# Edge layer of a four-layer image kernel: a quarter of one term on ScalarE, made a block ahead; the rest shared between VectorE and GpSimd

## The chip, the cores and the metric

The kernel runs on one core of a Trainium2 chip. A core has five engines with their own instruction queues: TensorE (PE in the profile, its weight loads PEld), VectorE (DVE), ScalarE (ACT), GpSimd (POOL) and SyncE (SP), which issues DMAs. Each queue runs in its own order, and an instruction waits until what it reads has been written and what it overwrites has been read. The metric is the device time of one execution in microseconds (us); shorter is better.

## The reference, cut to what matters

The program adds four layers to an image x of 4 x 56 x 56 x 128 numbers, each after a group norm. The change lies in the second layer alone:

```python
def _L1_conv_ref(x, We, be, Wn, bn):
    f = x.shape[-1]
    W1, W2 = (We[:, :f], We[:, f:])
    proj_i = jnp.einsum('blnf,of->blno', x, W1)
    proj_j = jnp.einsum('blnf,of->blno', x, W2)
    edge = jax.nn.relu(proj_i[:, :, :, None, :] + proj_j[:, :, None, :, :] + be)
    edge_sum = edge.sum(axis=3)
    node_in = jnp.concatenate([x, edge_sum], axis=-1)
    node = jax.nn.relu(jnp.einsum('blnc,oc->blno', node_in, Wn) + bn)
    return node
...
x = x + _L1_conv_ref(_gn(x), L1_conv_We, L1_conv_be, L1_conv_Wn, L1_conv_bn)
```

For every pixel n of an image row l and every of the 56 pixels m of the same row, an edge relu(proj_i[n] + proj_j[m] + be) is formed for each of 128 channels, and the edges are summed over m. That is 56 times as many numbers as the image has, so the work of the layer is in the element-wise edges and their sum.

## The kernel before, in words

The four samples go through the first two layers one after the other: `fast_layer` (layer 0) and then `edge_layer` (layer 1), four times each. `edge_layer` takes a sample as 7 blocks (`NBLK`) of 8 image rows, that is 448 pixels (`NB`). In a block the 128 channels are cut into four rows r of 32 channels, and the 56 partners m into four quarters of 14 (`M`), which lie on the four groups of 32 partitions. So one tile "128 x 1792" holds, for one m out of 14, all four rows r (4 x 448 elements) and on its partitions 32 channels for four partners at once. A block needs 14 such terms, and these are the 14 turns of the string `EDGE_TURNS` (`EDGE_END` in the last block).

- `project(j)`, TensorE: `e_pa`, the first projection of block j (four banks, one per row r), and `e_pc`, the negated second one.
- `evacuate(j, part)`, ScalarE: copies of these into SBUF, `e_a` (with the bias be added) and `e_c`; part 1 also adds bn to the sample (L1263).
- `terms(j, m, t, r0, r1, e)`: one term or some of its rows. For "d" VectorE forms max(a, c) in one instruction (L1273, tile `e_td`), reading c from PSUM. For "p" GpSimd forms a - c (L1275, tile `e_tp`) and ScalarE takes the relu in place (L1277). Since max(a, c) = relu(a - c) + c, what VectorE's terms have too much is summed per block into `e_rest` (two reduces, L1366 and L1367) and taken off by a matmul (L1360).
- A turn "s" is shared: rows 0 and 1 on VectorE (128 x 896), rows 2 and 3 on GpSimd and ScalarE.
- After each turn four matmuls per term (one per row r, L1344) sum it into `e_acc`, over partitions with a matrix of ones on four diagonals.
- At the end of a block ScalarE copies `e_acc` to `e_sums` (L1369), TensorE forms the node projection (`begun`, L1285, and `output`, L1291), and `finish` (L1296, VectorE) adds its relu to the sample. `finish(j - 2)` stands in VectorE's queue after turn 3 of block j, and in the last block `finish(j - 1)` after turn 9.
- `normed(j + 2)`, ScalarE, at turn 10: the group norm of a block to come (L1231).

`EDGE_TURNS` "ddpddpsdpdpddp" has 8 d, 5 p and 1 s; `EDGE_END` "ddpddpdpdpdddd" has 10 d and 4 p. Turns are counted from 0, so the p turns of a block are 2, 5, 8, 10 and 13; this text calls them p2 to p13, and s(j) is the shared turn (6) of block j.

The order on TensorE, ScalarE and VectorE is the order of the program text (`manual_schedule`). GpSimd's is not fixed by hand: the scheduler sets it. VectorE's full tiles have 7 buffers, GpSimd's 4, and the tiles of a shared turn 2.

Of the kernel before, what the change touches and what calls it, by code (L numbers as in the profile page):

```python
# [12 lines left out]
F32 = mybir.dt.float32  # L13
AF = mybir.ActivationFunctionType
ALU = mybir.AluOpType
AX = mybir.AxisListType
# [3 lines left out]
P = 128  # L20
B = 4
HH = 56
TOK = HH * HH
NB = 448
NBLK = TOK // NB
# [7 lines left out]
def bc(ap, axis, n):  # L33

    ap = ap.unsqueeze(axis)
    shape = list(ap.shape)
    shape[axis] = n
    return ap.to_broadcast(shape)


def blk(j):
    return slice(j * NB, (j + 1) * NB)
# [149 lines left out]
def apply_norm(k, out, xt, mr):  # L192
    k.nc.vector.tensor_scalar(out, xt, mr[:, 0:1], mr[:, 1:2], ALU.subtract, ALU.mult)
# [1004 lines left out]

EDGE_TURNS, EDGE_END = "ddpddpsdpdpddp", "ddpddpdpdpdddd"


def edge_layer(k, w, x1, st):
# [6 lines left out]
    nc, tc = k.nc, k.tc  # L1211
# [3 lines left out]
    with ExitStack() as es:  # L1215
        big = es.enter_context(tc.tile_pool(name="e_big", bufs=1))
        wk = es.enter_context(tc.tile_pool(name="e_wk", bufs=2))
# [7 lines left out]
        ready = {}  # L1225

        def normed(j):
            if j < 2:
                apply_norm(k, xg[:, blk(j)], xf[:, blk(j)], mr)
            elif j < NBLK:  # L1230
                nc.scalar.activation(xg[:, blk(j)], xf[:, blk(j)], AF.Identity, bias=shift, scale=mr[:, 1:2])  # L1231
# [22 lines left out]
        def evacuate(j, part):  # L1254
            if j >= NBLK:
                return
            pc, pa, c, a = ready[j]
            for r in range(2 * part, 2 * part + 2):
                nc.scalar.activation(a[:, r, :], pa[r][:, :NB], AF.Identity, bias=w.be[:, r:r + 1])
                if r == 0:  # L1260
                    nc.scalar.copy(c.rearrange("p r l m -> p (r l m)"), pc[:, :NB])  # L1261
            if part == 1:
                nc.scalar.activation(xf[:, blk(j)], xf[:, blk(j)], AF.Identity, bias=w.bn)  # L1263

        def terms(j, m, t, r0, r1, e):

            pc, _, c, a = ready[j]
            if e == "d":
                c = pc[:, :NB].rearrange("p (r l m) -> p r l m", r=4, l=8)
            cm = bc(c[:, r0:r1, :, m], 3, HH)  # L1270
            am = a[:, r0:r1, :].rearrange("p r (l n) -> p r l n", l=8)
            if e == "d":
                nc.vector.tensor_tensor(t, am, cm, ALU.max)  # L1273
            else:
                nc.gpsimd.tensor_sub(t, am, cm)  # L1275
                tf = t.rearrange("p r l n -> p (r l n)")
                nc.scalar.activation(tf, tf, AF.Relu)  # L1277

        def tile_of(e, n=4):
            return wk.tile([P, n, 8, HH], F32, tag="e_%s%d" % (e, n), name="e_t" + e,  # L1280
                           bufs=2 if n < 4 else 7 if e == "d" else 4)
# [16 lines left out]
        with tc.manual_schedule(engines={mybir.EngineType.PE, mybir.EngineType.Activation, mybir.EngineType.DVE}):  # L1298
            idle = psum.tile([P, 512], F32, tag="e_pc", name="e_idle", bufs=2)

            def fill(n):

                for _ in range(n):
                    nc.tensor.matmul(idle[:, :3 * P], k.ident, bc(k.ones, 1, 3), start=True, stop=True)
            mr = group_norm_factors(k, wk, bank, st, fill)
            nc.vector.tensor_scalar(shift, mr[:, 0:1], mr[:, 1:2], -1.0, ALU.mult, ALU.mult)
            for j in range(2):
                normed(j)
            project(0)
            for part in range(2):  # L1310
                evacuate(0, part)
            project(1)
            last = po = None
            for j in range(NBLK):
                end = j == NBLK - 1
                turns = EDGE_END if end else EDGE_TURNS
                nd, ns = turns.count("d"), turns.count("s")
                acc = psum.tile([P, 512], F32, name="e_acc")
                rest = wk.tile([P, 4, 8], F32, name="e_rest")
                at, ms = {"d": 0, "p": nd + ns, "s": nd}, []  # L1320
                for e in turns:
                    ms.append(at[e])
                    at[e] += 1
                early = {}
                if j == 0:
                    early = {g: tile_of(turns[g]) for g in
                             [g for g, e in enumerate(turns) if e == "d"][:3] + [turns.index("p")]}
                    for r in range(4):
                        for g, t in early.items():
                            terms(j, ms[g], t[:, r:r + 1], r, r + 1, turns[g])  # L1330
                for g, e in enumerate(turns):
                    m = ms[g]
                    if g in early:
                        parts = [(early[g], 0)]
                    elif e == "s":
                        parts = [(tile_of("d", 2), 0), (tile_of("p", 2), 2)]
                        for t, r in parts:
                            terms(j, m, t, r, r + 2, "p" if r else "d")
                    else:
                        parts = [(tile_of(e), 0)]  # L1340
                        terms(j, m, parts[0][0], 0, 4, e)
                    for t, r0 in parts:
                        for r in range(t.shape[1]):
                            nc.tensor.matmul(acc[quarters[r0 + r], :NB], w.S[:, 0, :], t[:, r].rearrange("p l n -> p (l n)"),  # L1344
                                             start=(g == 0), stop=(g == len(turns) - 1))
                    if g == 3 and po is not None:
                        finish(j - 2, po)
                    if g == 5:
                        evacuate(j + 1, 0)
                    if g == 7:  # L1350
                        evacuate(j + 1, 1)
                    if g == 10:
                        normed(j + 2)
                    if g == 6 and end:
                        po = output(*last)
                    if g == 9 and end:
                        finish(j - 1, po)
                    if g == 11:
                        for r in range(4):
                            nc.tensor.matmul(acc[quarters[r], :NB].rearrange("p (l n) -> p l n", l=8), w.S[:, 1, :],  # L1360
                                             bc(rest[:, r, :], 2, HH), start=False, stop=False)
                        if end:
                            po = begun(j)
                    if g == 8:
                        if ns:
                            nc.vector.tensor_reduce(rest[:, 0:2], ready[j][2][:, 0:2, :, 0:nd + 1], AX.X, ALU.add)  # L1366
                        nc.vector.tensor_reduce(rest[:, 2 if ns else 0:4], ready[j][2][:, 2 if ns else 0:4, :, 0:nd], AX.X, ALU.add)  # L1367
                sums = wk.tile([P, NB], F32, name="e_sums")
                nc.scalar.copy(sums, acc[:, :NB])  # L1369
                if end:  # L1370
                    idle = psum.tile([P, 512], F32, tag="e_pc", name="e_idle", bufs=2)
                    fill(2)
                if last and not end:
                    po = output(*last)
                project(j + 2)
                last = j, sums
            po = output(*last, po)
            fill(2)
            finish(NBLK - 1, po)
# [1476 lines left out]
def group_norm_factors(k, pool, bank, st, fill):  # L2856

    nc = k.nc
    mv = pool.tile([P, 2], F32, tag="mv", name="gf_mv")
    nc.vector.bn_aggr(mv, st.rearrange("p a b -> p (a b)"))  # L2860
    ps = bank()
    fill(2)
    nc.tensor.matmul(ps[:, 0:1], k.g4, mv[:, 0:1], start=True, stop=True)
    fill(1)
    mr = pool.tile([P, 2], F32, tag="mr", name="gf_mr")
    nc.vector.tensor_copy(mr[:, 0:1], ps[:, 0:1])
    t = pool.tile([P, 1], F32, tag="gt", name="gf_t")
    nc.vector.tensor_sub(t, mv[:, 0:1], mr[:, 0:1])
    nc.vector.tensor_mul(t, t, t)
    nc.vector.tensor_add(t, t, mv[:, 1:2])  # L2870
    ps = bank()
    nc.tensor.matmul(ps[:, 0:1], k.g4, t, start=True, stop=True)
    fill(1)
    nc.scalar.activation(t, ps[:, 0:1], AF.Sqrt, bias=k.eps)
    nc.vector.reciprocal(mr[:, 1:2], t)
    return mr
# [176 lines left out]
```

## Time and profile before

| What | Value |
|---|---|
| median of three runs | 3445.36 us (3444.44 to 3445.95) |
| the profiled execution: its time | 3443.31 us |
| the profiled execution: its span | 3441.5 us |
| mean granted TensorE clock | 0.997 |
| the four edge layers (from the first term to the last output) | 132.24, 132.19, 132.16, 132.30 us |
| busy per edge layer, mean: PE, DVE, ACT, POOL | 124.67, 125.56, 89.32, 120.11 us |

The span is what the profiler saw between the first and last instruction; the execution's own time has 1.8 us more around it. In the first sample the layer runs from 543.83 to 676.07 us; the blocks' first sums start at 549.69, 569.21, 588.94, 607.97, 625.76, 643.55 and 656.67 us. The other three samples show the same pattern within a few hundredths of a microsecond, so one is read and counted four times. A line of the timeline gives the start in us, the busy time in us, engine, source line, operation, output and inputs with their shapes, how many instructions were merged in the line, and in brackets the idle time before it with what ended it. Successive instructions on an engine overlap a little (a full tile's 3.26 us on POOL come 3.22 us apart, ScalarE's 1.70 us ones 1.60), so distances of starts are used where several follow each other.

### The profile page before, as it was taken

The page shows a single profiled execution, that of the slowest core. Times are in us where ns is not written, and L with a number is a line of the kernel's source. Part 1 is how long each engine was busy: PE and PEld are TensorE (multiplying, and loading weights), DVE is VectorE, ACT ScalarE, POOL GpSimd, SP SyncE. Part 2 cuts the span into 40 slices and gives each one's busy share as a digit, 9 for nine tenths or more (in the row PEclk, how much of TensorE's full clock was granted, in tenths as well). Part 3 has the DMA queues.
Part 4 walks back from the last instruction along what each step waited for, and adds up shares of the span by engine and source line. Part 5 has one row for each costly group of instructions (what it writes and reads, how often), then busy time and mean ns, then how long its engine had stood idle before and what let it go on. Part 6 is the DMA issues. An engine that isn't in the chain of part 4 may idle for free. (4 is left out here: it accounts for less than half of the span.)

```text
span 3441.5 us, 64526 instructions
## 1 busy us (share of the span) xinstructions
PE 3317.2 (96%) x27834; PEld 1425.6 (41%) x27834; DVE 2651.4 (77%) x2552; ACT 2134.0 (62%) x2257; POOL 1284.9 (37%) x795
## 2 busy tenths in 40 slices
PE   7999999999999999999999999999999999999998
PEld 4433333353333435333343443333437443336664
DVE  6588877867888597788859858887785878895776
ACT  4688876668888575788867668887564013215442
POOL 1000007800000491000019500000685978884786
PEclk9999999999999999999999999999999999999999
DMA  2143420024344000444320034442104047743111
GB/s 107 45 93 90 97 54 20 20 51 96 88 93 89 20 1 20 102 97 97 87 48 5 20 74 93 97 91 61 38 12 110 2 96 186 189 112 94 57 20 57
DMA packets 97868, 243.42 MB, mean 71 GB/s; under 512 B 64440, under 2 KB 69816, under 8 KB 92440
## 3 DMA queue, kind: packets, MB, share of 16 engines
q0 software_dynamic: 16128, 102.77, 14.9%
q1 hardware_dynamic: 74728, 123.61, 12.3%
q10 hardware_dynamic: 6720, 12.85, 1.4%
q8 instruction: 220, 3.60, 0.4%
q14 instruction: 72, 0.59, 0.1%
HBM read 79.43 MB, written 31.33 MB: 32 GB/s over the span
## 5 line engine op out<-in xcount | busy, mean ns | idle before, releaser
L830 ACT ACTIVATE f_ring<-f_pm 128x1792 f32<-128x1792 f32 (+1 forms) x764 | 1093.8, 1482 | 226.6 <-PE f_pm L827 179.1
L682 DVE TENSOR_TENSOR f_acc<-f_acc,f_ring 128x1792 f32<-128x1792 f32 x468 | 947.7, 2025 | 191.4 <-ACT f_ring L830 161.1
L827 PE MATMUL f_pm<-f_qT,f_kT 32*128 32x448 f32 x5376 | 722.8, 571 | 9.9 <-ACT f_p L716 4.1
L672 POOL DMA_DIRECT2D f_far<-f_ring x112 | 96.5, 862 | 1327.5 <-ACT f_ring L830 1012.3
L693 PE MATMUL f_pm<-f_ring,f_va 128*32 128x448 f32 (+1 forms) x6304 | 589.4, 490 | 0.0
L1275 POOL TENSOR_TENSOR e_tp<-e_a,e_c 128x1792 f32<-128x1792 f32 (+2 forms) x172 | 480.3, 2833 | 33.4 <-issue 33.4
L1273 DVE TENSOR_TENSOR e_td<-e_a,e_pc 128x1792 f32<-128x1792 f32 (+2 forms) x292 | 478.4, 1706 | 8.8 <-ACT e_c L1261 8.8
L827 PEld LDWEIGHTS f_pm<-f_qT,f_kT 32*128 32x128 f32 x5376 | 260.1, 183 | 411.8 <-ACT f_ring L830 301.1
L693 PEld LDWEIGHTS f_pm<-f_ring,f_va 128*32 128x32 f32 x6304 | 163.9, 109 | 410.1 <-issue 397.8
L1277 ACT ACTIVATE e_tp<-e_tp 128x1792 f32<-128x1792 f32 (+2 forms) x172 | 253.3, 1495 | 98.0 <-POOL e_tp L1275 98.0
L2040 DVE TENSOR_TENSOR u_ud<-u_px,u_d 112x1792 f32<-112x1792 f32 x144 | 263.5, 1863 | 39.9 <-PE u_po L2045 35.4
L2042 POOL TENSOR_TENSOR u_up<-xh,u_d 112x1792 f32<-112x1792 f32 (+1 forms) x72 | 240.9, 3374 | 56.0 <-PE u_po L2045 39.7
L1344 PE MATMUL e_acc<-e_td,t_edge 128*32 128x448 f32 x1952 | 231.6, 542 | 6.6 <-DVE e_td L1273 6.4
L2045 PE MATMUL u_po<-u_ud,AT 112*64 112x448 f32 x1056 | 212.4, 541 | 0.5 <-DVE u_ud L2040 0.5
L1344 PE MATMUL e_acc<-e_tp,t_edge 128*32 128x448 f32 x1184 | 148.0, 543 | 23.6 <-ACT e_tp L1277 23.6
L2045 PEld LDWEIGHTS u_po<-u_ud,AT 112*64 112x64 f32 x1056 | 74.0, 137 | 126.5 <-issue 112.6
L1344 PEld LDWEIGHTS e_acc<-e_td,t_edge 128*32 128x32 f32 x1952 | 61.8, 110 | 142.4 <-issue 93.8
L737 DVE RECIPROCAL f_den<-f_den 128x448 f32<-128x448 f32 x28 | 82.6, 2951 | 44.5 <-ACT f_den L734 44.5
L1874 POOL TENSOR_TENSOR q_u<-iS,q_g 128x1792 f32<-128x1792 f32 x32 | 104.3, 3287 | 12.2 <-PE q_acc L1889 12.2
L813 POOL TENSOR_TENSOR x<-xf,xw 128x343 f32<-128x343 f32 x28 | 25.5, 909 | 222.1 <-DVE xf L802 222.1
L2145 ACT COPY x_ev<-x_po 56x896 f32<-56x896 f32 x32 | 28.8, 900 | 125.1 <-DMA x_xs<-xat 69.9
L1889 PE MATMUL q_acc<-q_u,S 64*64 64x448 f32 x1024 | 101.2, 540 | 2.1 <-DVE y L1908 1.1
(535 smaller groups left out, 4575.7 us busy)
## 6 DMA issues: line engine op xcount, KB each, us to landing
f_far<-f_ring POOLq DMA_DIRECT2D x112, 896.0 KB, 6.4
u_d<-dd SPq DMA_DIRECT2D x46, 784.0 KB
f_far<-f_ring SPq DMA_DIRECT2D x28, 896.0 KB
xw<-in_x SPq DMA_DIRECT2D x4, 1568.0 KB
x2d<-x SPq DMA_DIRECT2D x4, 1568.0 KB
xat<-x SPq DMA_DIRECT2D x4, 1568.0 KB
x_xs<-xat ACTq DMA_DIRECT2D x32, 196.0 KB
xm<-x_ev ACTq DMA_DIRECT2D x64, 98.0 KB
```

The source lines that it names most:

```text
L682: nc.vector.tensor_add(e.acc, e.acc, slots(j, c))
L693: nc.tensor.matmul(e.po[heads[h], part], va[o, c, heads[h]], p, start=(c == 0), stop=(c == 23 and part.stop == NB))
L827: nc.tensor.matmul(ss[:, i, :NB], kT[heads[h], c * P:(c + 1) * P], qT[heads[h], blk(j)], start=True, stop=True)
L830: nc.scalar.activation(ring[:, slot:slot + m, :], ss[:, :m, :NB], AF.Exp, scale=scale)
L1273: nc.vector.tensor_tensor(t, am, cm, ALU.max)
L1275: nc.gpsimd.tensor_sub(t, am, cm)
L1277: nc.scalar.activation(tf, tf, AF.Relu)
L1344: nc.tensor.matmul(acc[quarters[r0 + r], :NB], w.S[:, 0, :], t[:, r].rearrange("p l n -> p (l n)"), start=(g == 0), stop=(g == len(turns) ...
L1874: nc.gpsimd.tensor_mul(u, bc(st.iS[:, bp, c, :HH], 1, HEADS), bc(g[:, n, c, :], 2, HH))
L2040: nc.vector.tensor_mul(u, bc(px[:, :, :NB], 2, m), dm)
L2042: nc.gpsimd.tensor_mul(u, bc(x, 2, m), dm)
L2045: nc.tensor.matmul(po[64 * b2:64 * b2 + 64, :NB], st.AT[:, 8 * i + h0 + q, 2 * bp + b2, :], u[:, b2, q, :], start=(left == 16), stop=(left ...
```

## The change

In every block but the first, row 3 of the shared term is made by ScalarE alone and a block ahead: `single(j + 1, m)` forms less = -c for the eight image rows (one ACTIVATE on 128 x 8) and then eight ACTIVATEs of 128 x 56, relu(a + less), into a tile `e_a1`. It is issued in two lots, at turn 10 (less and four) and turn 12 (the other four) of block j. Rows 0 to 2 of the shared term go to VectorE up to `split` and to GpSimd from there: in odd blocks 2 rows and 1, in even blocks 1 and 2, in the last block 3 and none, in block 0 (which has no row made ahead) 2 and 2 as before. In the last block turn 6 was a full "d" and becomes "h", a shared one. The reduces of `e_rest` follow `split`.

```diff
-EDGE_TURNS, EDGE_END = "ddpddpsdpdpddp", "ddpddpdpdpdddd"
+EDGE_TURNS, EDGE_END = "ddpddpsdpdpddp", "ddpddphpdpdddd"
...
+        def single(j, m):
+
+            t = tile_of("a", 1)
+            _, _, c, a = ready[j]
+            less = wk.tile([P, 8], F32, name="e_less")
+            nc.scalar.activation(less, c[:, 3, :, m], AF.Identity, scale=-1.0)
+            for l in range(8):
+                nc.scalar.activation(t[:, 0, l, :], a[:, 3, HH * l:HH * (l + 1)], AF.Relu, bias=less[:, l:l + 1])
+                if l == 3:
+                    yield t
+            yield t
...
-                nd, ns = turns.count("d"), turns.count("s")
+                nd, ns = turns.count("d"), turns.count("s") + turns.count("h")
+                split = 3 if end else 1 + j % 2 if j else 2
...
-                    elif e == "s":
-                        parts = [(tile_of("d", 2), 0), (tile_of("p", 2), 2)]
-                        for t, r in parts:
-                            terms(j, m, t, r, r + 2, "p" if r else "d")
+                    elif e in "sh":
+                        parts = [(made, 3)] if j else []
+                        for e, r0, r1 in ("d", 0, split), ("p", split, 3 if j else 4):
+                            if r0 < r1:
+                                parts.append((tile_of(e, 3)[:, :r1 - r0], r0))
+                                terms(j, m, parts[-1][0], r0, r1, e)
...
                     if g == 10:
                         normed(j + 2)
+                        if not end:
+                            work = single(j + 1, (EDGE_END if j == NBLK - 2 else EDGE_TURNS).count("d"))
+                    if g in (10, 12) and not end:
+                        made = next(work)
...
                     if g == 8:
-                        if ns:
-                            nc.vector.tensor_reduce(rest[:, 0:2], ready[j][2][:, 0:2, :, 0:nd + 1], AX.X, ALU.add)
-                        nc.vector.tensor_reduce(rest[:, 2 if ns else 0:4], ready[j][2][:, 2 if ns else 0:4, :, 0:nd], AX.X, ALU.add)
+                        nc.vector.tensor_reduce(rest[:, :split], ready[j][2][:, :split, :, 0:nd + 1], AX.X, ALU.add)
+                        nc.vector.tensor_reduce(rest[:, split:], ready[j][2][:, split:, :, 0:nd], AX.X, ALU.add)
```

More of the change, by code (lines that the diff above doesn't have):

```diff
@@ L1316, in edge_layer @@
                 turns = EDGE_END if end else EDGE_TURNS
-                nd, ns = turns.count("d"), turns.count("s")
+                nd, ns = turns.count("d"), turns.count("s") + turns.count("h")
+                split = 3 if end else 1 + j % 2 if j else 2
                 acc = psum.tile([P, 512], F32, name="e_acc")
                 rest = wk.tile([P, 4, 8], F32, name="e_rest")
-                at, ms = {"d": 0, "p": nd + ns, "s": nd}, []
+                at, ms = {"d": 0, "p": nd + ns, "s": nd, "h": nd}, []
                 for e in turns:
```

## The prediction

> **What bounds the kernel now.** The change touches four equal stretches, the edge layers, so I first read the busy time of each engine in the first of them and in a block out of its middle (block 4). Columns: the stretch and its length, then busy time of PE, PEld, DVE, ACT, POOL.
>
> ```profile
> core 0: us, PE busy (x) PEld busy (x) DVE busy (x) ACT busy (x) POOL busy (x), PEclk, DMA share, GB/s
> 543.83:676.07 132.24, 124.66 (x1118) 44.49 (x1117) 125.54 (x93) 89.36 (x96) 120.11 (x44) 1.00 0.01 1
> 619.95:637.75 17.80, 17.43 (x169) 6.59 (x165) 17.54 (x13) 13.28 (x14) 17.80 (x7) 1.00 0.01 2
> ```
>
> POOL is busy for the whole of the block, DVE all but 0.26 us, PE nearly; ACT has 4.5 us free. POOL's timeline shows that it never pauses from the first term on, and where it puts the shared half tile:
>
> ```profile
> 543.93 120.12 POOL L1275 TENSOR_TENSOR e_tp<-e_a,e_c 128x448 f32<-128x448 f32 x43 [8.32 <-issue]
> ...
> 630.12 1.73 POOL L1275 TENSOR_TENSOR e_tp<-e_a,e_c 128x896 f32<-128x896 f32 x1
> 631.80 3.27 POOL L1275 TENSOR_TENSOR e_tp<-e_a,e_c 128x1792 f32<-128x1792 f32 x1
> ```
>
> The half at 630.12 is s(5), one block early: ScalarE's relu of s(4) was over long before. The tile at 631.80 is p13 of block 4. A POOL block is 5 x 3.22 + 1.69 = 17.79 us, the distance of PE's blocks 3, 4 and 5 (607.97, 625.76, 643.55). What follows in block 4 on ScalarE, from p5's relu to the next block's p2:
>
> ```profile
> 623.75 1.70 ACT L1277 ACTIVATE e_tp<-e_tp 128x1792 f32<-128x1792 f32 x1 [1.52 <-POOL e_tp L1275]
> ...
> 632.41 0.78 ACT L1231 ACTIVATE e_xg<-x,e_shift,gf_mr 128x448 f32<-128x448 f32 x1
> 635.10 1.70 ACT L1277 ACTIVATE e_tp<-e_tp 128x1792 f32<-128x1792 f32 x1 [1.91 <-POOL e_tp L1275]
> 637.88 0.53 ACT L1369 COPY e_sums<-e_acc 128x448 f32<-128x448 f32 x1 [1.08 <-PE e_acc L1344]
> 638.32 1.70 ACT L1277 ACTIVATE e_tp<-e_tp 128x1792 f32<-128x1792 f32 x1
> ```
>
> The reader should see that p13's relu starts when POOL is done with it, and that ScalarE waits there for 1.91 us. That relu releases TensorE's last turn, which ends the block:
>
> ```profile
> 636.86 0.96 PE L1344 MATMUL e_acc<-e_tp,t_edge 128*32 128x448 f32 x8 [0.36 <-ACT e_tp L1277]
> ```
>
> The turn before started at 635.55 and undisturbed turns come 0.75 us apart, so PE loses 0.56 us here: its own floor is 17.79 - 0.56 = 17.23 us per block. The output of the block then releases `finish` on VectorE:
>
> ```profile
> 639.55 0.68 DVE L1296 SCALAR_TENSOR_TENSOR x<-e_po,e_nbn,x 128x448 f32<-128x448 f32 x1 [0.27 <-PE e_po L1291]
> ...
> 657.00 0.68 DVE L1296 SCALAR_TENSOR_TENSOR x<-e_po,e_nbn,x 128x448 f32<-128x448 f32 x1
> ...
> 664.29 0.68 DVE L1296 SCALAR_TENSOR_TENSOR x<-e_po,e_nbn,x 128x448 f32<-128x448 f32 x1 [0.43 <-PE e_po L1291]
> ```
>
> From 639.55 VectorE runs to its last term (672.70) with one pause of 0.43. So the path is POOL from 543.93 to p13 of block 4, then ScalarE, TensorE, and VectorE to the end. Only the blocks up to 4 count for POOL: its end at 664.05 is 8.7 us before VectorE's.
>
> **The change, part by part.** *POOL.* A quarter costs 953 ns in its rows (the x16 of 128x448), a half 1726; starts are 0.91 and 1.69 apart, so a quarter for a half saves 0.77. That holds for s(1), s(3), s(5). Before p5(4) lie s(1) and s(3): POOL is 0.76 us early from block 1, 1.53 from block 3, 2.29 from block 5 on. Its buffers allow it: p13(4) overwrites the tile of p2(4), which TensorE read by 628.1, 3.7 us earlier.
>
> *VectorE.* 2012, 1080 and 615 ns for full, half and quarter: 0.47 per row. It saves a row in s(2), s(4) and in turn 6 of the last block. The first two only widen its pauses (0.95, 1.50, 0.26, 0.27 before the finishes of blocks 0 to 3); I count them at nothing on that cover, and without it they would be worth 0.9 more. The third lies behind 639.55, where VectorE sets the pace: -0.4, after which TensorE, not VectorE, is last at that turn. The last block's reduce becomes two: a second one costs some 0.2 (275 ns busy, 0.2 apart) and falls into the pause of 0.43. The other blocks have two already. At the end of the layer no wait is new.
>
> *TensorE.* The same four matmuls per turn, the made row first in the shared turn: nothing.
>
> *ScalarE.* Nine small ACTIVATEs per block made ahead. No row shows a series of 128x56 with a per-partition bias from SBUF. Nearest rows:
>
> ```profile
> L1643 ACT ACTIVATE s_d<-s_d,c_eps 128x56 f32<-128x56 f32 x4 | 1.3, 335 | 0.0
> ```
>
> ```profile
> 3121.77 0.30 ACT L2480 ACTIVATE o_r<-o_s,c_eps 128x7 f32<-128x7 f32 x1
> 3121.98 0.38 ACT L2481 ACTIVATE o_r<-o_s,eps,factors 128x7 f32<-128x7 f32 x1
> ```
>
> The same shape is busy for 335 ns; an ACTIVATE with a bias, busy 300, lets the next start after 210, so 90 overlap. From below: 0.20 each (9 x 0.20 = 1.8); from above: 335 without overlap (3.0), since the first must wait for `less`. I take 0.24, the same shape with the overlap seen: 9 x 0.24 = 2.16 us. Where the cover is gone is p13: relu p5 to the end of `normed` is 632.41 + 0.70 - 623.75 = 9.36 of unbroken ScalarE work; both lots then stand ahead of p13's relu. In even blocks p13 is ready for ScalarE at 9.36 + 2.16 = 11.52 after p5, against 635.10 - 623.75 = 11.35 by POOL before; in odd blocks the relu of s shrinks by 0.37: 11.15. Queued behind: p13's relu, the block's sums, the next p2; TensorE's last turn waits for them. Until p5 ScalarE has caught up again: 11.52 + 3.22 (635.10 to 638.32) + 1.60 = 16.34, under POOL's 17.02 to 17.79.
>
> **The Trainium skill**, ScalarE: Activation LUTs, "What ACT_TABLE_LOAD costs", gives an ACTIVATE with a bias operand 280 ns + 0.833 per element and 93 of overlap: 327 - 93 = 234 for 56 elements, nine of them 2.1; L1643's 335 agrees, and the sum would be 0.05 better per layer. Its "Rules for kernel authors" speaks against the change: relu and max belong on VectorE, not ScalarE. As engine time that is so (VectorE's quarter 615 ns, or 470 as part of a tile, against eight ACTIVATEs); were busy time the measure, each block would lose about 1.5 us and the four layers 36. Here it counts what each engine has free.
>
> **The sum**, first layer, shifts against before:
> - Blocks 0 and 1, whose p13 POOL delivered 9.7 after p5 (the half came later), lose on it: block 1 has p13 at 569.6 + 11.15 = 580.8 for 580.05. TensorE ends block 1 0.3 late; its waits in block 2 (0.27, 1.03) take that up.
> - Block 2: p5 at 588.17 - 0.76 = 587.41, p13 at 598.93 for 599.52: -0.59.
> - Block 3: POOL allows -1.53; TensorE's floor, -0.59 - 0.54 (its loss at this turn), allows -1.13.
> - Block 4: -1.53 + 0.17 = -1.36 (TensorE's floor would allow -1.69). VectorE's finish of block 3 follows: -1.36 (VectorE itself would allow -1.6).
> - Last block: -0.4.
>
> Together -1.76 per layer, four layers -7.0: 3443.31 - 7.0 = 3436.3 for the profiled execution. The median of the runs lies 2.05 above that execution, so 3438.3 us.
>
> **Rivals.** *The whole saving arrives:* POOL's 2.29 and the last block's 0.4 all reach the end, 4 x 2.7 = 10.8: 3434.6. For it: POOL is the only engine without a pause. Against: it needs the lots at 0.20 or less, and TensorE has 0.56 to give per block.
>
> *The lots eat it:* at 335 ns each the lots take 3.0, p13(4) comes 1.53 - 1.01 = 0.5 early, the layer gains 0.9: 3445.36 - 3.7 = 3441.7. For it: the dependence on `less`. Nearer zero still if GpSimd's order, which nobody fixes, puts a quarter behind p8: ScalarE's queue then stands for 1.1.
>
> *Slower: ScalarE becomes the bound.* Its loop is 9.36 + 3.22 + 1.60 = 14.18 plus the lots (13.81 in odd blocks). Above 3.7, or 0.41 per small ACTIVATE, it exceeds POOL's 17.79 and the delay carries over from block to block. At 0.50 (something between each pair that the rows don't show) the loop is 18.5 and five blocks lose 0.7 each, 4 x 3.5 = 14 us: 3459. For it: no row has such a series. Against: 335 ns is the longest of that shape.
>
> *The change doesn't do what it says:* only GpSimd's order is open; it can't undo 0.77 less work.
>
> **How the numbers follow.** Forecast (gain of 4.5 to 9 us): 0.60; the whole saving: 0.10; eaten (within 4.5): 0.14; slower: 0.16. Predicted 3438.3. The likeliest case's own range is 3436 to 3441. The range goes down to 3434 (10.8 with half a microsecond) and up to 3445.5 (no gain), which leaves out the slower case and little else. A measurement of this kernel can tell about 0.2% (6.9 us) from no change. Of the forecast's 0.60 I put 0.42 beyond 6.9, because VectorE's 0.9 in s(2) and s(4) and the shorter lots are counted at nothing: faster 0.52, within 0.32, slower 0.16.
>
> **What would show it.** Right: POOL's series falls from 120.1 to about 117.8 per layer, small ACTIVATEs start 0.2 to 0.26 apart, p13's relu in block 4 follows the second lot without a pause, the layer lasts 130.5. Wrong: small ACTIVATEs 0.3 or more apart, p2's and p5's relus late against POOL, a TensorE wait for `e_a` or for a shared tile at turn 6, VectorE pausing before the last block.

## The result, and the profile after

| What | Before | After |
|---|---|---|
| median of the runs | 3443.62 us (13 runs, 3441.84 to 3445.95) | 3451.97 us (13 runs, 3448.34 to 3456.53) |
| the profiled execution: its time, its span | 3443.31, 3441.5 us | 3451.95, 3450.1 us |
| mean granted TensorE clock | 0.997 | 0.994 |
| edge layer, first VectorE term to the end of the last `finish`, mean of four | 132.80 us | 130.97 us |
| end of the fourth layer's last `finish` | 2577.72 us | 2570.04 us |
| from there to the first matmul of `u_po`, the next step's output | 207.59 us | 222.74 us |
| from that matmul to the end of the span | 656.2 us | 657.3 us |

The changed kernel takes 1.0024 times as long, 95% interval 1.0017 to 1.0031: slower by 0.24%. The forecast was 3438.3, so it was wrong in sign and by 13.7 us. The table already says where: the edge layers gave 1.83 us each, 7.3 in all (1.76 and 7.0 were forecast), the fourth ended 7.7 us earlier, and 15.2 us went in a stage behind them that the diff doesn't touch.

**The layer.** Busy time by stretch in the changed kernel, the first layer and its block 4, with the columns of the prediction's first view; then GpSimd's series from its timeline:

```profile
core 0: us, PE busy (x) PEld busy (x) DVE busy (x) ACT busy (x) POOL busy (x), PEclk, DMA share, GB/s
543.47:673.84 130.37, 123.23 (x1118) 44.77 (x1117) 124.10 (x94) 99.91 (x150) 117.82 (x44) 1.00 0.01 1
618.00:635.60 17.60, 17.45 (x172) 6.54 (x164) 17.60 (x14) 15.24 (x23) 17.60 (x8) 1.00 0.01 2
```

```profile
543.57 117.83 POOL L1275 TENSOR_TENSOR e_tp<-e_a,e_c 128x448 f32<-128x448 f32 x43 [8.32 <-issue]
```

GpSimd is down from 120.12 to 117.83, ScalarE up by 10.6, and the layer shorter. ScalarE's timeline in block 4, around the two lots (L1284 makes `less`, L1286 the row):

```profile
630.52 0.77 ACT L1231 ACTIVATE e_xg<-x,e_shift,gf_mr 128x448 f32<-128x448 f32 x1
631.17 0.22 ACT L1284 ACTIVATE e_less<-e_c 128x8 f32<-128x8 f32 x1
631.43 1.97 ACT L1286 ACTIVATE e_ta<-e_a,e_less 128x56 f32<-128x56 f32 x8
633.30 1.69 ACT L1277 ACTIVATE e_tp<-e_tp 128x1792 f32<-128x1792 f32 x1
636.07 0.53 ACT L1387 COPY e_sums<-e_acc 128x448 f32<-128x448 f32 x1 [1.08 <-PE e_acc L1359]
```

Nine small ACTIVATEs take 631.17 to 633.30, 2.13 us, and p13's relu follows them without a bracket: it used to wait 1.91 us for GpSimd, now it waits for ScalarE's own queue. That is the picture the prediction drew.

**Behind the layer.** The last layer's sample goes through a further group norm while the stage `spectra` begins and GpSimd prepares weights for two later steps: the score weights (`t_w_qk`, `q_g`, `q_t`) and the value weights (`t_w_V`, `t_w_P`, `d_d`, `d_t`). Busy time by stretch there, changed kernel and, below, the kernel before:

```profile
2589.00:2599.00 10.00, 9.82 (x206) 9.33 (x206) 8.02 (x37) 3.73 (x8) 9.80 (x17) 1.00 0.70 252
2599.00:2609.00 10.00, 2.89 (x36) 2.67 (x32) 9.54 (x4) 1.54 (x3) 10.00 (x14) 0.77 0.01 2
2609.00:2619.00 10.00, 7.49 (x66) 5.31 (x68) 7.27 (x9) 2.41 (x6) 9.82 (x13) 0.50 0.00 0
2619.00:2629.00 10.00, 10.00 (x160) 8.83 (x157) 4.38 (x14) 4.00 (x9) 1.42 (x2) 0.87 0.58 158
```

```profile
2599.00:2609.00 10.00, 10.00 (x215) 9.75 (x212) 7.89 (x31) 3.12 (x8) 9.82 (x15) 1.00 0.02 3
2609.00:2619.00 10.00, 10.00 (x162) 8.39 (x162) 6.52 (x16) 6.19 (x16) 8.17 (x8) 1.00 0.08 30
```

In the second stretch VectorE is "busy" for 9.54 us with 4 instructions, TensorE for 2.89, and the granted clock falls to 0.77 and then 0.50 (means of these stretches; in single microseconds it is 0.50 from 2605 to 2621 and 1.00 again from 2622). VectorE's and TensorE's timelines show the instructions:

```profile
2600.13 3.55 DVE L1601 TENSOR_TENSOR s_t<-s_mv,s_mr 128x1 f32<-128x1 f32 x1
2603.72 7.74 DVE L1602 SCALAR_TENSOR_TENSOR s_t<-s_t,s_mv 128x1 f32<-128x1 f32 x1
2611.38 0.61 DVE L232 COPY xh<-s_px 112x448 f32<-112x448 f32 x1
...
2612.21 2.86 DVE L1613 TENSOR_TENSOR s_d<-s_rows 128x56 f32<-128x56 f32 x1
```

```profile
2611.51 0.59 PE L1606 MATMUL s_pt<-s_t,t_shared 128*128 128x1 f32 x2 [9.62 <-DVE s_t L1602]
```

One element per partition in 7.74 us: these instructions don't work, they are held. The same three in the kernel before:

```profile
2608.52 0.40 DVE L1583 TENSOR_TENSOR s_t<-s_mv,s_mr 128x1 f32<-128x1 f32 x1
2608.95 0.22 DVE L1584 SCALAR_TENSOR_TENSOR s_t<-s_t,s_mv 128x1 f32<-128x1 f32 x1
...
2610.52 1.47 DVE L1595 TENSOR_TENSOR s_d<-s_rows 128x56 f32<-128x56 f32 x1
```

GpSimd's timeline around the holds in the changed kernel:

```profile
2588.18 0.25 POOL L1806 TENSOR_TENSOR t_w_qk<-t_w_qk,t_w_qkr 128x32 f32<-128x32 f32 x1 [9.21 <-DMA t_w_qkr<-in_w_qkr]
...
2601.11 0.24 POOL L1812 TENSOR_TENSOR t_w_qk<-t_w_qk,q_skip 128x32 f32<-128x32 f32 x1
...
2602.41 1.25 POOL L1821 TENSOR_TENSOR q_t<-t_w_qk 128x512 f32<-128x512 f32 x1
2603.65 0.36 POOL L1811 TENSOR_SCALAR q_skip<-t_images 128x32 f32<-128x32 f32 x1
2603.98 0.24 POOL L1820 TENSOR_TENSOR q_g<-t_w_qk 128x32 f32<-128x32 f32 x1
2604.19 1.12 POOL L1784 TENSOR_TENSOR d_t<-t_w_P,t_w_V 128x448 f32<-128x448 f32 x1
2605.27 1.25 POOL L1822 TENSOR_TENSOR q_g<-q_g,q_t 128x512 f32<-128x512 f32 x1
...
2610.59 0.24 POOL L1821 TENSOR_TENSOR q_t<-t_w_qk 128x32 f32<-128x32 f32 x1
2610.82 1.40 POOL L1792 TENSOR_SCALAR d_t<-t_w_V,t_images 128x448 f32<-128x448 f32 x1
```

L1601 ends at 2603.68, when GpSimd comes to a TENSOR_SCALAR (one input and a scalar), and L1602, which starts 0.07 us after that one did, at 2611.46, in GpSimd's next TENSOR_SCALAR. In between GpSimd runs an unbroken row of instructions with two inputs, alternately of the score weights (q) and the value weights (d). Why they stand there now is seen in SyncE's queue (start of an issue, its length, what is loaded), changed kernel first, then before:

```profile
2575.43 0.32 SPq L3009 DMA_DIRECT2D xw<-xad  x1
2575.79 0.79 SPq L158 DMA_DIRECT2D t_w_qk<-in_w_qk  x1
2583.80 0.32 SPq L3009 DMA_DIRECT2D xw<-xad  x1
2584.18 0.41 SPq L158 DMA_DIRECT2D t_w_qkr<-in_w_qkr  x1
```

```profile
2577.17 0.90 SPq L158 DMA_DIRECT2D t_w_qk<-in_w_qk  x2
2578.11 0.69 SPq L158 DMA_DIRECT2D t_w_qkr<-in_w_qkr  x1
2579.16 0.33 SPq L158 DMA_DIRECT2D t_w_V<-in_w_V  x1
2583.11 0.33 SPq L2991 DMA_DIRECT2D xw<-xad  x1
```

The order of SyncE's and GpSimd's queues is the scheduler's. After the edit it has put the two halves of the next image (`xw`, which wait for TensorE to have read the old one) ahead of `t_w_qkr`, so that this load goes out 6.1 us later though the layer ends 7.7 us earlier. GpSimd waits 9.21 us for it (first line of its timeline above), and its work for both weights then falls beside the norm, in another order. On TensorE, VectorE and ScalarE the order of the instructions traced in the 100 us behind the layer is the same in both kernels.

### The profile page after: what moved, and what is told of

It reads as the page before. It is cut to its first block, busy times and chain, and to the rows that moved or that the text cites. A ratio compares the mean times of both kernels' runs of the same rounds, so it can differ in the third digit from the quotient of the medians.

```text
span 3450.1 us, 64715 instructions
## 1 busy us (share of the span) xinstructions
PE 3320.4 (96%) x27834; PEld 1434.7 (42%) x27834; DVE 2657.5 (77%) x2556; ACT 2176.7 (63%) x2473; POOL 1276.1 (37%) x795
## 5 line engine op out<-in xcount | busy, mean ns | idle before, releaser
L1275 POOL TENSOR_TENSOR e_tp<-e_a,e_c 128x1792 f32<-128x1792 f32 (+2 forms) x172 | 471.3, 2779 | 33.4 <-issue 33.4
L1273 DVE TENSOR_TENSOR e_td<-e_a,e_pc 128x1792 f32<-128x1792 f32 (+3 forms) x292 | 472.9, 1688 | 8.8 <-ACT e_c L1261 8.8
```

## The experiments

Medians are in us, and the ratio is to runs of the kernel before that lay beside (their medians are 3442.60 to 3443.62); "stage" is the time from the end of the fourth layer's last `finish` to the first `u_po` matmul, and "longest" the longest of the norm's small VectorE instructions, both from the profiled execution.

| Kernel | median | ratio to before, 95% | layer | stage | longest |
|---|---|---|---|---|---|
| before | 3443.62 | | 132.80 | 207.6 | 1.47 |
| after | 3451.97 | 1.0017 to 1.0031 | 130.97 | 222.7 | 7.74 |
| e1 after, queue of before | 3436.68 | 0.9971 to 0.9989 | 130.95 | 208.8 | 1.18 |
| e3 before, queue of after | 3455.85 | 1.0023 to 1.0051 | 132.83 | 219.7 | 7.42 |
| e2 after, two instructions on ScalarE | 3446.71 | 1.0003 to 1.0021 | 130.98 | 220.8 | 6.84 |
| e9 after, score weights ahead | 3435.34 | 0.9970 to 0.9994 | 130.97 | 210.9 | 1.17 |
| e10 after, value weights ahead | 3434.90 | 0.9968 to 0.9991 | 130.97 | 207.7 | 1.35 |
| e11 after, groups apart | 3436.88 | 0.9976 to 1.0001 | 130.94 | 207.6 | 1.30 |
| e5 = e1, two rows on VectorE | 3434.41 | 0.9964 to 0.9984 | 130.31 | 209.5 | 1.21 |
| e6 = e1, no shared turn at the end | 3440.66 | 0.9984 to 1.0003 | 131.36 | 209.7 | 1.24 |
| e7 = e1, lots apart | 3438.28 | 0.9969 to 0.9990 | 130.31 | 209.7 | 1.26 |
| e8 = e5 and e7 | 3432.16 | 0.9963 to 0.9985 | 129.40 | 208.4 | 1.18 |

**Undoing the order alone (e1) and making it alone (e3).** The theory (Q, the queue): the whole loss is the order of the queues. Dependencies that wait for nothing and only fix the order of issue pin SyncE's loads, in e1 to the order before on the changed kernel, in e3 to the changed order on the kernel before. In e1 GpSimd's order followed of itself.

```diff
+def queue_order(k, names):
+    names = names.split()
+    for a, b in zip(names, names[1:]):
+        k.tc.add_manual_dep(k.sp[b].ins, k.sp[a].ins.name,
+                            mybir.DependencyInfo(mybir.DependencyClass.NoSync, mybir.DependencyReason.DATA),
+                            reason="queue_order")
...
                     spectra(k, w2, st, xat, images, bulk)
+                    queue_order(k, "qk4 qk qkr V x20 Vrev P x2d x21 dd W b nb")
```

In e3 the string is "qk4 x20 qk x21 qkr V Vrev P x2d W b nb M0 M0rev M1 M1rev ms dd" (x20 and x21 are the two halves of `xw`).

> The changed kernel, with nothing altered but the order of the weight loads and image loads on SyncE's queue behind the last edge layer, pinned to the order of the kernel before (GpSimd's order there then comes out as before too). Theory Q (the edge layers gained what was forecast, and the scheduler's other order of SyncE's loads behind them costs about 15 us): 3443.6 - 7.5 = 3436 us, ratio 0.9978; TensorE's pause of 9.6 us and the clock of 0.50 in the spectra stage are gone. Rival L (the loss is not in that order, but in the new instructions themselves, their queue or memory places): stays near 3452, ratio 1.002.

> The kernel before, with nothing altered but the same queue's order, pinned to the order of the changed kernel. Theory Q: 3443.6 + 15.5 = 3459 us, ratio 1.0045, with a TensorE pause of some 10 us in the spectra stage. Rival L: 3443.6, ratio 1.000.

Measured: e1 3436.68, 15.3 us under the changed kernel and 6.8 under the one before; e3 3455.85, 0.37% above the one before, with three instructions of the norm at 4.06, 7.42 and 2.95 us and TensorE pauses of 2.56 and 5.64 where one of some 10 was expected. With the layers as they were in each (130.95 and 132.83), the order alone unmakes all of the loss and makes most of it (the stage is 12.1 us longer in e3, 15.2 in the changed kernel). e1 is also 1.6 from the forecast, and its gain 6.8 where 7.0 was forecast: this is the kernel that was predicted.

**Moving the two held instructions (e2).** The two 128x1 instructions of the norm go to ScalarE, in the last sample alone; queues as in the changed kernel.

```diff
-    nc.vector.tensor_sub(t1, mv[:, 0:1], mr[:, 0:1])
-    nc.vector.scalar_tensor_tensor(t1, t1, t1, mv[:, 1:2], ALU.mult, ALU.add)
+    if b == B - 1:
+        nc.scalar.activation(t1, ps[:, 0:1], AF.Square, bias=mv[:, 0:1], scale=-1.0)
+        nc.scalar.activation(t1, t1, AF.Identity, bias=mv[:, 1:2])
+    else:
...
```

> The changed kernel with its own queue order; in the last sample's image norm the two VectorE instructions on 128x1 numbers with two SBUF inputs each, which took 3.55 and 7.74 us, are replaced by two ScalarE ACTIVATEs (square of the difference, then the sum). Theory S (VectorE's small two-input instructions were held up by GpSimd's two-input series beside them, and that is what stopped TensorE): the pause of 9.6 us and the low clock go, 3437 to 3442 us. Rival W (TensorE would have waited there for GpSimd's late score weights anyway): 3450 or more. In between, if the next two-input instruction of the norm, on 128x56, is held up in its place.

Measured: 3446.71, a third of the loss back (its profiled execution, 3452.7, lies 6 above its median). The hold moved to the next instructions with two inputs from SBUF: `s_d` lasted 2.22 and `s_sq` 6.84 us. The first ends 0.13 us into a TENSOR_SCALAR of GpSimd, the second 0.10 before one begins. So it isn't those two instructions, but whatever of this kind stands beside that row.

**The hold by itself (e4).** The kernel before, with one more VectorE instruction in block 3 of each edge layer, whose result nothing uses; its operands differ from layer to layer. In the edge layer GpSimd runs terms without a pause.

```diff
+            if k.layers == 0:
+                nc.vector.tensor_sub(t[:, 0:1], mr[:, 0:1], shift)
+            elif k.layers == 1:
+                nc.vector.tensor_sub(t[:, 0:1], mr[:, 0:1], pc[:, 0:1])
+            elif k.layers == 2:
+                nc.vector.tensor_scalar(t[:, 0:1], shift, mr[:, 0:1], mr[:, 1:2], ALU.subtract, ALU.mult)
+            else:
+                nc.vector.tensor_sub(t, a[:, 0, :], a[:, 1, :])
```

> The kernel before with one additional VectorE instruction per edge layer, in block 3 after turn 4, where GpSimd runs its two-input subtractions without a pause; its result is used by nobody. Layer 1: 128x1 with two SBUF inputs; layer 2: 128x1 with one SBUF and one PSUM input; layer 3: 128x1 with one SBUF input and two per-partition scalars; layer 4: 128x448 with two SBUF inputs. Theory S: layer 1 takes microseconds (up to the next gap in GpSimd's series, 3 us or more) where such an instruction takes 0.16 beside an idle GpSimd, layer 4 is held up as well, layers 2 and 3 take 0.16 to 0.3. Rival: all four take what they take elsewhere, 0.16, 0.16, 0.2 and 0.6. By theory Q the additional instruction may also change the scheduler's order behind the layers; then this run shows the 10 us pause as well and is some 10 to 20 us above the kernel before.

VectorE's timeline, the four added instructions, and GpSimd's around the first:

```profile
606.54 13.98 DVE L1304 TENSOR_TENSOR e_probe<-gf_mr,e_shift 128x1 f32<-128x1 f32 x1
...
1252.98 0.15 DVE L1306 TENSOR_TENSOR e_probe<-gf_mr,e_pc 128x1 f32<-128x1 f32 x1
...
1886.36 0.27 DVE L1308 TENSOR_SCALAR e_probe<-e_shift,gf_mr 128x1 f32<-128x1 f32 x1
...
2520.85 14.44 DVE L1310 TENSOR_TENSOR e_probe<-e_a 128x448 f32<-128x448 f32 x1
```

```profile
599.50 21.00 POOL L1275 TENSOR_TENSOR e_tp<-e_a,e_c 128x1792 f32<-128x1792 f32 x7
626.89 3.25 POOL L1275 TENSOR_TENSOR e_tp<-e_a,e_c 128x1792 f32<-128x1792 f32 x1 [6.39 <-PE e_acc L1358]
```

Two inputs from SBUF: held for 13.98 and 14.44 us, past the ends of four terms. The first hold ends when GpSimd's row does, at 620.50 (GpSimd then waits 6.39 us for TensorE to free a tile). One input from PSUM: 0.15. So of the two 128x1 TENSOR_TENSORs the one is held and the other not, with the place of one operand as the difference; the kernel's own terms, which read c from PSUM, are not held beside the same row. The one run of this kernel took 3491.57 us: the two layers with a hold last 146.04 and 146.51 us, the other two 132.8 as before. The added instructions also changed SyncE's order behind the layers to that of the changed kernel; there the norm was held again (4.18, 7.73 and 2.85 us), and TensorE paused for 10.24 us. So one added instruction per edge layer can turn that order.

The Trainium skill, SBUF — State Buffer, "SBUF: two separate sides", names the mechanism: a VectorE instruction with two SBUF inputs and a GpSimd instruction that reads SBUF need the same pair of ports, which the first one gets for the whole of its instruction while the other is blocked. That the instruction with one SBUF input passes agrees with e4. That the wait lasts for one instruction of the other side does not: 13.98 us are more than four terms of 3.26, and in the changed kernel 7.74 us are eleven GpSimd instructions. The next runs ask when it is one and when it is many.

**Lateness or company (e9, e10).** Is it that the score weights come late, or what stands beside the norm? On the changed kernel, one more string each: e9 "qkr x20", which brings the loads of `t_w_qk` and `t_w_qkr` ahead of the image; e10 "qk4 V Vrev P x20 qk x21 qkr", which brings those of the value weights ahead and leaves the score weights late.

> The changed kernel with its own SyncE order but for one dependency: the loads of t_w_qk and t_w_qkr stand ahead of the image's two halves; those of t_w_V, t_w_Vrev and t_w_P stay behind them. GpSimd then makes the score weights first and all of the value weights' instructions after, some 18 us of them. Theory (what costs is GpSimd's two-input series standing beside the last norm's small VectorE instructions, each of which is held until GpSimd comes to a one-input instruction): the score part is over near 2598 us, the value part then stands beside the norm, with a stretch of five two-input instructions (5.6 us) in it: one or two small instructions of some 3 to 6 us, part of the loss stays, 3440 to 3447. Rival (the loss is the lateness of the score weights themselves, which GpSimd waits 6.6 and 9.2 us for): all of it comes back, 3437.

> The reverse: t_w_V, t_w_Vrev and t_w_P ahead of the image's halves, t_w_qk and t_w_qkr behind them as in the changed kernel. GpSimd makes the value weights first, and the score weights, late as in the changed kernel, stand alone beside the norm; between their two-input instructions a one-input one comes every 1.5 to 2.8 us. Theory of the held-up instructions: no small VectorE instruction lasts over about 3 us, most of the loss is gone, 3437 to 3441. Rival (late score weights): 3449 to 3452 as in the changed kernel.

Both lost the whole penalty: 3435.34 and 3434.90 (medians; one of the ten runs of each took 3452.26 and 3450.04). e10 refutes lateness: `t_w_qkr` is behind the image, GpSimd begins the score weights at 2596.78, and the stage is as short as ever. But e9 refutes the theory's size as well: five two-input instructions of the value weights (2600.35 to 2605.92) did stand beside the norm, and L1601 and L1602 lasted only 1.12 and 1.05 us: each got in at the end of the GpSimd instruction that was running. VectorE's timeline in e9:

```profile
2602.63 1.12 DVE L1601 TENSOR_TENSOR s_t<-s_mv,s_mr 128x1 f32<-128x1 f32 x1
2603.79 1.05 DVE L1602 SCALAR_TENSOR_TENSOR s_t<-s_t,s_mv 128x1 f32<-128x1 f32 x1
```

What the slow kernels have and e1, e9 and e10 have not is the alternation of the two groups in that row.

**The groups apart (e11).** The changed kernel with its own SyncE order, now pinned, and one dependency on GpSimd: the value weights' first instruction behind the score weights' last.

```diff
-    nc.gpsimd.tensor_add(half[:, 0, :], w.V[0:32, 0, 0, :], w.Vrev[:, 0, :])
+    k.sp["first_d"] = nc.gpsimd.tensor_add(half[:, 0, :], w.V[0:32, 0, 0, :], w.Vrev[:, 0, :])
...
-    nc.gpsimd.tensor_scalar_mul(st.g4[:, 1], st.g4[:, 1], k.qm4[:, 4:5])
+    k.sp["last_q"] = nc.gpsimd.tensor_scalar_mul(st.g4[:, 1], st.g4[:, 1], k.qm4[:, 4:5])
...
+                    queue_order(k, "qk4 x20 qk x21 qkr V Vrev P x2d W b nb M0 M0rev M1 M1rev ms dd")
+                    queue_order(k, "last_q first_d")
```

> The changed kernel with its own SyncE order, loads as late as in it (t_w_qkr last), and one dependency on GpSimd: the value weights' instructions start after the score weights' last one, so that the two groups no longer alternate. Theory after the last two runs (a small VectorE instruction is held past the end of GpSimd's current instruction only where the two groups alternate; within one group it gets in at the next instruction): no instruction of the last norm lasts over about 1.5 us, TensorE's pause is gone, and the total is 3435 to 3438. Rival (any late GpSimd series beside the norm does it): one of them lasts over 3 us and the total stays above 3443.

VectorE's timeline and below it GpSimd's:

```profile
2599.94 1.30 DVE L1601 TENSOR_TENSOR s_t<-s_mv,s_mr 128x1 f32<-128x1 f32 x1
2601.28 0.23 DVE L1602 SCALAR_TENSOR_TENSOR s_t<-s_t,s_mv 128x1 f32<-128x1 f32 x1
...
2602.05 1.07 DVE L1613 TENSOR_TENSOR s_d<-s_rows 128x56 f32<-128x56 f32 x1
...
2608.80 1.06 DVE L1626 TENSOR_SCALAR s_mean<-s_mean,s_mr 128x56 f32<-128x56 f32 x1
2609.78 1.16 DVE L1628 SCALAR_TENSOR_TENSOR s_t<-s_mr 128x1 f32<-128x1 f32 x1
```

```profile
2588.84 0.25 POOL L1806 TENSOR_TENSOR t_w_qk<-t_w_qk,t_w_qkr 128x32 f32<-128x32 f32 x1 [10.79 <-DMA t_w_qkr<-in_w_qkr]
...
2601.20 0.36 POOL L1811 TENSOR_SCALAR q_skip<-t_images 128x32 f32<-128x32 f32 x1
...
2602.97 0.27 POOL L1812 TENSOR_TENSOR t_w_qk<-t_w_qk,q_skip 128x32 f32<-128x32 f32 x1
...
2608.68 1.13 POOL L1783 TENSOR_TENSOR d_d<-t_w_P,d_m 128x448 f32<-128x448 f32 x1
2609.78 1.14 POOL L1786 TENSOR_TENSOR d_d<-t_w_P,d_m 128x448 f32<-128x448 f32 x1
2610.89 1.13 POOL L1785 TENSOR_TENSOR d_d<-d_d,d_t 128x448 f32<-128x448 f32 x1
```

3436.88 (one of its ten runs took 3455.25): the loads are as late as in the changed kernel (GpSimd waits 10.79 us), the row stands beside the norm, and yet nothing is held for more than 1.30: L1626 ends at 2609.86 and L1628 at 2610.94, where one GpSimd instruction ends and the next begins. The order of the loads, of TensorE, VectorE and ScalarE is that of the changed kernel, only GpSimd's row differs: what costs is its alternation. How the alternation keeps VectorE out stays open. It isn't the kind of the two neighbours: in the changed kernel GpSimd goes from L1822 to L1812, both of the score weights, at 2601.11, and L1601, waiting since 2600.13, doesn't get in, while in e11 L1613 gets in between the same two at 2602.97. Nor is it a matter of coming in time: L1602 starts 0.07 us after the TENSOR_SCALAR L1811 in both kernels, and lasts 0.23 us in e11 and 7.74 in the changed one. And in e4 terms of one kind alone held an instruction past four ends.

**The layer's terms (e5 to e8), all on e1.** Edits of three places: e5 GpSimd's part one row in blocks 1 to 5; e6 the last block as before; e7 the first lot at turn 12, the second at turn 4 of the block itself; e8 is e5 and e7 together.

```diff
-                split = 3 if end else 1 + j % 2 if j else 2
+                split = 3 if end else 2
...
-EDGE_TURNS, EDGE_END = "ddpddpsdpdpddp", "ddpddphpdpdddd"
+EDGE_TURNS, EDGE_END = "ddpddpsdpdpddp", "ddpddpdpdpdddd"
...
-                    if g in (10, 12) and not end:
+                    if g == 12 and not end or g == 4 and j:
                         made = next(work)
```

> The changed kernel with SyncE's order of before (as in the first experiment, 3436.7 us, layer 130.3), and in every block from 1 to 5 two rows of the shared term on VectorE and one on GpSimd (GpSimd's half becomes a quarter in blocks 2 and 4 too). Theory of the layer as in the prediction (the path is POOL up to p13 of block 4, then VectorE): POOL's terms up to p13(4) are 2 x 0.77 = 1.5 us shorter, but TensorE's floor and VectorE, which gets 0.47 back in blocks 2 and 4, take most of it: layer about 129.8, total 3434.6. Rival (VectorE is now the bound from block 1 on, so its rows decide): two rows more on VectorE make the layer 2 x 0.47 longer, 131.2, total 3440.4.

> The changed kernel with SyncE's order of before, and the last block as in the kernel before (turn 6 a full VectorE term, no row made ahead for it). If the last-block term of the sum is right, the layer is 0.4 us longer than with it (130.7 for 130.3) and the total 3436.7 + 1.6 = 3438.3. Rival: the pace of the last block is TensorE's, not VectorE's: nothing changes, 3436.7.

> The changed kernel with SyncE's order of before, and ScalarE's two lots moved: the first to turn 12 of the block ahead, the second to turn 4 of the block itself, where ScalarE waits for GpSimd anyway (1.52 us ahead of p5's relu in the kernel before). If the lots delay p13's relu by about 0.17 us, as the sum has it, the layer is 0.1 to 0.2 shorter (130.1 to 130.2) and the total 3436.0. Rival: the lots are hidden already: no difference, 3436.7. GpSimd's order in block 1 changes by one place with it (the half for block 2 one tile earlier), which should cost nothing.

> Both edits together: two rows of every shared term on VectorE and one on GpSimd, and ScalarE's lots at turns 12 and 4. If both terms are right, 129.6 us per layer and 3434.0 in all, the fastest of the study; if VectorE is the bound, 131.2 and 3440.

The medians of these four can't be read to 2 us (e7's runs go from 3430.7 to 3439.9), the layers can: in each kernel its four agree within 0.1 us. Start of each block's `e_sums` copy after the layer's first term, first layer:

```
block     0      1      2      3      4       5       6
before  21.21  39.44  58.47  76.26  94.05  111.27  129.95
e1      22.35  39.91  57.78  75.00  92.58  109.80  128.06
e5      22.35  39.65  56.87  74.10  91.32  108.54  127.45
e7      21.41  38.70  56.94  74.73  91.96  109.18  127.44
e8      21.41  38.69  56.18  73.40  90.62  107.85  126.53
```

e6: the layer is 0.41 longer, as the last-block term said; its median is 4.0 above e1's, 2.3 more than four such layers explain. e5: 0.64 shorter; blocks 2 to 5 take 17.22 to 17.23 each, with no pause of TensorE (over 0.08 us) in them: this is TensorE's floor, and the rival (VectorE the bound) falls. e7: 0.64 shorter where 0.1 to 0.2 was expected, the miss of this set: it is 1.21 ahead of e1 at block 1 (38.70 for 39.91), 0.27 at block 3 and 0.62 from block 4 on (the section after this one says from what). e8: 1.55 shorter than e1, its blocks 3 to 5 on TensorE's floor, and the fastest kernel of the study, 3432.16, 11.0 under the kernel before that ran with it (3443.17).

## Why the prediction was wrong

- *The sum per layer* held: 1.76 forecast, 1.83 measured, 7.3 in four. The block table (e1 against before) holds its steps too: by -0.59 at block 2 (-0.69 measured), -1.13 at block 3 (-1.26), -1.36 at block 4 (-1.47), and -0.4 more in the last block (-0.42; e6 takes away 0.41).
- *ScalarE's lots*: 2.16 forecast, 2.13 measured. So neither "the lots eat it" nor "ScalarE becomes the bound"; VectorE's pause of 0.43 before the last `finish` but one stayed, and hid the second reduce.
- *Blocks 0 and 1* were mis-sized: the sum had 0.3 late at block 1. Measured: 1.14 late at block 0, where TensorE's last turn waits 1.13 us for p13's relu behind the lots (0.20 in e7, with only the first lot ahead of it), and 0.47 at block 1. There the relu follows not the lots but, after a wait of 0.18, GpSimd, which puts the half for block 2 ahead of p13; in e7 the half stands behind, and p13 is done 1.68 us earlier (35.43 for 37.11 after the first term). So e7 moved two things, the lots and one place in GpSimd's order. Block 2 took the delay up, as the sum said.
- *The lots in block 4* were mis-sized too, though their length was right: the sum lost 0.17 to them. In e1 block 4 takes 17.58 us, and p13's relu follows the lots without a pause; in e7, with only the first lot ahead of it, the block takes 17.23, TensorE's floor. That is 0.35, twice as much, and with the 0.27 that e7 is ahead at block 3 nearly all of its gain. At block 4 the sum had -1.36, and -1.69 as the most that TensorE's floor allows; e1 has -1.47, but e7 -2.09: the floor moves with the blocks ahead of it.
- *The step that failed* is the rival "*The change doesn't do what it says:* only GpSimd's order is open; it can't undo 0.77 less work", with the sum's silent term that all outside the four layers stays as it was. The order that is open is that of every queue the scheduler sets, SyncE's too, and over the whole program. In its place the runs showed: a changed order of SyncE's loads behind the last layer (e1, e3), through it an alternating row of GpSimd instructions (e11), a norm held by it for 3.55 and 7.74 us, and a TensorE that paused for 9.62 us and ran at a granted clock of 0.50 for some 10 us after (from 2611.51 to between 2621 and 2622). The pause and half of these 10 us make 14.6, an estimate; the stage is 15.2 longer, against 7.7 won before it.
- *The chances*: 0.16 for slower were all put on ScalarE as the bound, a case that the trace excludes; the case that came was priced at nothing, though the text said itself that the scheduler sets GpSimd's order.

## What to carry to other kernels

An edit is priced with the queues that nobody fixes, far behind the edited lines: compare the instruction order of the two builds on every engine before believing that the rest is unchanged, and pin an order that is worth something with dependencies that only order. Where a tiny VectorE instruction lasts for microseconds, look at what GpSimd runs beside it. Here an operand from PSUM passed (e4), and keeping two independent groups on GpSimd from alternating gave all of the loss back (e11); moving two instructions to ScalarE gave back a third, since the next ones were held in their place (e2). And judge a small edit by the stage it touches as well as by the total: here the layer was right to 0.1 us while the total went the other way.

## What the runs showed of the hardware

- A VectorE instruction of 128x1 with two SBUF inputs lasted 13.98 us beside GpSimd's edge terms, and 0.15 with one input from PSUM. A TENSOR_SCALAR of 128x1 with two scalars from SBUF passed once in 0.27 (e4); one of 128x56 with one scalar (L1626) lasted 1.06 and 1.18 beside the value weights (e11, e1), and 0.25 in the changed kernel, where GpSimd was done by then.
- Of the eleven holds of over 2 us beside the norm (changed kernel, e2, e3, e4) nine end 0.02 to 0.74 us after GpSimd starts a TENSOR_SCALAR, and two 0.02 and 0.10 before. But not every TENSOR_SCALAR ends one: L1613 in the changed kernel (2612.21 to 2615.07) was passed by one of 0.35 us (2613.51).
- A hold lasts to the end of the running GpSimd instruction in some rows (1.05 to 1.30 us in e9 and e11) and past three to eleven of them in others (3.55 to 14.44 us).
- In TensorE's pause (2601.89 to 2611.51) the granted clock was 1.00 up to 2604, 0.73 from 2604 to 2605 and then 0.50; it stayed so until 2621, 9.5 us after TensorE had begun again without a pause, was 0.74 in the next microsecond and 1.00 from 2622. The Trainium skill, TensorE: Matmul & The Clock Gate, "What's actually happening", says that the clock is halved after an idle window of about 3.4 us and restored after one or more busy ones. The halving agrees; here it came 2.1 to 3.1 us after the last matmul, sooner than a whole window, and the return took 9.5 to 10.5 us of TensorE at work.
